# Two-layer decoder on one core: expert results written by token with indirect DMAs, and context units moved behind the expert tiles' branches

## The chip, the cores and the metric

The kernel runs on one core of a Trainium2 chip. The metric is the device time of one execution in microseconds (us), the median of several runs. TensorE (PE) multiplies matrices, VectorE (DVE), ScalarE (ACT) and GpSimd (POOL) do the rest of the arithmetic, and SyncE (SP) issues most DMAs. Each engine works through its own queue in order.

## What is computed

A decoder of two layers on x of 32 sequences x 128 tokens x 256 features, all in float32, with a context of the same shape. Each step adds its result to x, and each takes a layernorm of x first:

```python
x = x + L0_attn(layernorm(x))                    # latent attention, 16 heads
x = x + L0_xattn(layernorm(x), ctx)              # cross attention with position bias
x = x + L0_ffn(layernorm(x))                     # 8 experts, each token goes to the best 2
x = x + L1_attn(layernorm(x))                    # gated recurrence in chunks of 64, then an MLP
x = x + L1_xattn(layernorm(x), ctx)              # one head, keys and values of ctx
x = x + L1_ffn(layernorm(x))                     # ternary weights, 8-bit activations, 3-tap convolution
```

The expert step is the one that matters here. For each token, `w` are the softmax weights of the two best experts, and

```python
out = sum_e w[e] * (relu(x @ W1[e] + b1[e]) @ W2[e] + b2[e])   # 256 -> 1024 -> 256
```

The layer-1 cross attention needs keys `ctx @ W_lk.T + b_lk` and values `ctx @ W_lv.T + b_lv`, which depend on the inputs alone.

## The kernel before, in words

The program is written in a framework that orders each engine's instructions by its own time model and sets the semaphores. `keep_in_program_order` pins an instruction behind the one that was written before it on its engine; all matmuls and most transposes are pinned (helper `mm`, line 206, and `turned`, line 209), so TensorE's order is that of the text. Tracked dependencies are by tile and by region of a DRAM tensor.

**Attention, then routing.** x stays in SBUF throughout. After both attentions, `route` writes the normed rows to the DRAM tensor `xs` and picks two experts per token. `phase_c` sorts the 8192 pairs of token and expert into slots: each expert gets whole tiles of TS = 256 slots, 39 tiles at most (NT). Sixty-four small matmuls (line 781) turn the slots round into `who`, the token of each slot (line 786); `slots` (line 787) holds the two slots of each token.

**Contexts.** NU = 16 units of two sequences (U = 2, T = 256 tokens). `context(u)` gives three pieces: `load` (256 KB of transposed ctx into `cT`, line 666), `keys` (8 matmuls into `ck`, then ScalarE, line 677) and `values` (8 matmuls into `cv`, then VectorE, line 686, and a 512 KB store to the DRAM tensor `ckv`, line 690). Units 0 to 5 (CTX0 = 6) run before the expert tiles, units 6 to 15 in layer 1.

**Expert tiles.** For tile j: `brought` loads its expert's weights (2.2 MB into `moe`, line 800, two buffers) and gathers 2 x 128 rows of `xs` by `who` with indirect DMAs on GpSimd (`xr`, line 807, six buffers, so three tiles); `tokens` transposes them (copy at line 820); `first_layer` has 32 matmuls `h` and ReLU on ScalarE (line 832); `second_layer` has 32 matmuls `y` and the bias on VectorE (line 844), and stores the tile to its place in `ys` with one plain DMA (line 845). On TensorE the order is h of tile j, transposes of tile j+1, y of tile j. 36 tiles (`some`) always run, the last three only when `tiles > j`, which each engine tests on a register (loaded at line 862) in a branch. In the profiled execution 36 ran. The places of the three are filled with zeros before (line 854).

**Layer 1.** 16 units go through a chain of some 60 pieces each. PLAN gives the round of each piece, and each unit starts STEP = 11 rounds after the one before; eight or nine units are under way at a time. A unit begins with `gather` (four indirect DMAs from `ys` by `slots`, line 1054, pinned on GpSimd), and `added` (round 3, line 1063) adds them to x with the routing weights `rw`. Then come `d_stats`, `d_nb`, `d_norm` and `d_scaled` (a norm, its result `hn_d`), `d_flip` (transpose `pt_d`, copied by ScalarE into `hT_d`) and the projections `d_q` and so on, the scan (lines 1139 to 1145, with `u_d` of line 1113 on GpSimd), `m_y` (the output projection). The `kv_e` load of the context (line 1198) comes in round 32 and has two buffers, released by `lv_e` (line 1260). In the last step `f_taps` has a GpSimd addition (`z_f`, line 1320) between two ScalarE operations, and `f_out` stores x (line 1371).

The ten contexts of layer 1 are spread over its rounds by a table written by hand, three rounds for each unit:

```python
    CTX_ROUNDS = (
        (0, 0, 0), (0, 1, 1), (0, 2, 2), (0, 3, 3), (1, 4, 5), (2, 6, 7), (4, 9, 9), (6, 12, 12),
        (9, 14, 15), (12, 16, 17),
    )
```

In a round, contexts come ahead of the units' pieces. Their weights `wc` (line 1382, 512 KB) and those of the attention itself, `we` (line 942, 512 KB), are loaded at the start of layer 1.

Of the kernel before, what the change touches and what calls it, by code (L numbers as in the profile page):

```python
# [10 lines left out]
F32 = mybir.dt.float32  # L11
# [6 lines left out]
P = 128  # L18
# [4 lines left out]
G = 4  # L23
# [38 lines left out]
RV = {"b_vv": (0, D), "b_lv": (D, D), "br": (2 * D, NE), "bo": (2 * D + NE, D)}  # L62
RV_A = RV["bo"][0]


# [10 lines left out]
def decoder(ctx: ExitStack, tc: tile.TileContext, a: dict, out: bass.AP):  # L76
# [70 lines left out]
    def stats(src, name):  # L147
        st = small.tile([P, G, 6], F32, tag="st", name=f"st_{name}")
        mv = small.tile([P, G, 2], F32, tag="mv", name=f"mv_{name}")
        for i in range(G):  # L150
            V.bn_stats(st[:, i, :], src[:, i, :])
            V.bn_aggr(mv[:, i, :], st[:, i, :])
        return mv
# [66 lines left out]
    xs = dram.tile([NTOK, D], F32, name="xs")  # L220
    ys = dram.tile([NT * TS, D], F32, name="ys")
    U = 2
# [3 lines left out]
    rw = keepc.tile([P, 2, NB], F32, name="rw")  # L226
    slots = keepc.tile([P, 2, NB], I32, name="slots")
    wm = keepc.tile([P, 2], F32, name="wm")
    wq = keepc.tile([P, 2, 2048], BF16, name="wq")

    routed = ExitStack()
    keepr = routed.enter_context(tc.tile_pool(name="route", bufs=1))
# [12 lines left out]
    def attention():  # L245
        with tc.tile_pool(name="pa", bufs=2) as pool, tc.tile_pool(name="pa1", bufs=1) as keep:
# [329 lines left out]
            def route(g):  # L576
# [10 lines left out]
                for i in range(G):  # L587
                    for c in range(2):
                        mm(p3[:, i, :], xT[:, c, i * S : (i + 1) * S], W("r", 2)[:, c, :], c == 0, c == 1)
                sm = lambda t, sh=(P, G, NE): small.tile(list(sh), F32, tag=f"r_{t}", name=f"{t}_{n}", bufs=2)  # L590
                lg = sm("lg")
# [67 lines left out]
    def context(u, wcs, turned_tile, kv_tile):  # L659

        wc = wcs.rearrange("p (w c m) -> p w c m", w=2, c=2)
        t = {}

        def load():
            t["cT"] = turned_tile(f"cT_k{u}")
            nc.sync.dma_start(
                out=t["cT"], in_=a["ctxT"][:, u * T : (u + 1) * T].rearrange("(c p) t -> p c t", p=P)
            )

        def keys():  # L670
            t["kv"] = kv_tile(f"kvc_{u}")
            p = bank(f"ck_{u}").rearrange("p (c t) -> p c t", c=2)
            for c in range(2):
                for k in range(2):
                    mm(p[:, c, :], wc[:, 0, k, c * P : (c + 1) * P], t["cT"][:, k, :], k == 0, k == 1)
            for c in range(2):
                A.activation(
                    t["kv"][:, 0, c * T : (c + 1) * T], p[:, c, :], AF.Identity, bias=vec("b_lk")[:, c : c + 1]
                )

        def values():
            p = bank(f"cv_{u}").rearrange("p (i d) -> p i d", i=U)
            for i in range(U):
                for c in range(2):
                    mm(p[:, i, :], t["cT"][:, c, i * S : (i + 1) * S], wc[:, 1, c, :], c == 0, c == 1)
            V.tensor_tensor(
                t["kv"][:, 1].rearrange("p (i d) -> p i d", i=U), p,
                row("b_lv")[:, None, :].to_broadcast([P, U, D]), ALU.add,
            )
            nc.sync.dma_start(out=ckv[u], in_=t["kv"])  # L690

        return load, keys, values

    def load_d():
# [7 lines left out]
    def phase_c():  # L702
        with tc.tile_pool(name="pc", bufs=2) as pool, tc.tile_pool(name="pc1", bufs=1) as keep:
            wcs = keep.tile([P, E_W // 2], F32, name="wc")
# [61 lines left out]
            V.scalar_tensor_tensor(rowp, col, -float(P), sl, ALU.mult, ALU.add)  # L766
            pk = bank("tokens")
            F16 = mybir.dt.float16
            for t in range(0, NB, G):
                for j in range(2):  # L770
# [8 lines left out]
                    for i in range(G):  # L779
                        A.activation(c[:, i, :], c[:, i, :], AF.Copy, scale=conr("tok")[:, t + i : t + i + 1])  # L780
                        PE.matmul(
                            pk[:, :NJ], lhsT=o[:, i, :], rhs=c[:, i, :],
                            start=t + i + j == 0, stop=t + i == NB - 1 and j == 1,
                        )
            who = k("who", (NJ,), I32)
            V.tensor_scalar(who, pk[:, :NJ], float(NTOK // 2), None, ALU.add)
            V.tensor_copy(slots, sl)

            for u in range(CTX0):
                for piece in context(  # L790
                    u, wcs, lambda n: pool.tile([P, 2, T], F32, tag="cT", name=n, bufs=4),
                    lambda n: pool.tile([P, 2, U * D], F32, tag="kv", name=n, bufs=4),
                ):
                    piece()
            wf = keep.tile([P, 4096], F32, name="wf")

# [38 lines left out]
            def second_layer(t):  # L835
# [4 lines left out]
                for h in range(TS // P):  # L840
# [3 lines left out]
                    V.tensor_tensor(yt[:, h, :], y[:, :D], b2, ALU.add)  # L844
                nc.sync.dma_start(
                    out=ys[j * TS : (j + 1) * TS, :].rearrange("(h p) d -> p h d", h=TS // P), in_=yt
                )


            some = 2 * NTOK // TS + NE // 2  # L850
            none = keep.tile([P, TS // P * D], F32, name="none")
            GP.memset(none, 0.0)
            for j in range(some, NT):
                nc.sync.dma_start(
                    out=ys[j * TS : (j + 1) * TS, :].rearrange("(h p) d -> p h d", h=TS // P),
                    in_=none.rearrange("p (h d) -> p h d", h=TS // P),
                )
            tiles = nc.values_load(end_i[0:1, 0:1], min_val=0, max_val=NT)
# [8 lines left out]
            for j in range(some):  # L867
# [7 lines left out]
                if j == 3:  # L875
                    ternary(wf, keep)
                    for c in range(2):
                        for part, v in (
# [3 lines left out]
                            A.activation(part, part, AF.Copy, scale=vec(v)[:, c : c + 1])  # L882
            rest(some)
        return wd

    def ternary(wf, keep):
# [23 lines left out]
    PLAN = (  # L910
        (0, "gather0 gather1"), (1, "gather2 gather3"), (3, "added"), (4, "d_stats"), (5, "d_nb"),
        (6, "d_norm"), (7, "d_scaled"), (8, "d_flip"), (10, "d_q d_a"), (11, "d_k d_g d_scan1"),
        (13, "d_v d_q2"), (14, "d_rms d_scan2"), (15, "d_state"), (16, "d_gate"), (18, "m_y"),
# [10 lines left out]

    CTX0 = 6
    CTX_ROUNDS = (
        (0, 0, 0), (0, 1, 1), (0, 2, 2), (0, 3, 3), (1, 4, 5), (2, 6, 7), (4, 9, 9), (6, 12, 12),
        (9, 14, 15), (12, 16, 17),
    )

    def layer1(wd):
# [8 lines left out]
        with tc.tile_pool(name="pl", bufs=1) as pool, tc.tile_pool(name="pl1", bufs=1) as keep:  # L940
            wes = keep.tile([P, E_W // 2], F32, name="we")
            nc.sync.dma_start(out=wes, in_=a["we"][:, : E_W // 2])
            we = wes.rearrange("p (w c m) -> p w c m", w=2, c=2)
# [99 lines left out]
            def unit(u):  # L1043
# [4 lines left out]

                def gather(k):
                    t = u * U + k % U  # L1050
                    o["yr", k] = pool.tile([P, D], F32, tag="yr", name=f"yr_{t}_{k // U}", bufs=5)

                    tc.keep_in_program_order(
                        GP.indirect_dma_start(
                            out=o["yr", k], out_offset=None, in_=ys[:, :],
                            in_offset=bass.IndirectOffsetOnAxis(ap=slots[:, k // U, t : t + 1], axis=0),
                        )
                    )

                def added():  # L1060
                    for k in range(2 * U):
                        t, i = u * U + k % U, k % U
                        V.scalar_tensor_tensor(
                            x[:, i, :], o.pop(("yr", k)), rw[:, k // U, t : t + 1], x[:, i, :], ALU.mult, ALU.add
                        )

# [80 lines left out]
                def d_state():  # L1147
                    V.tensor_tensor(o["pre"], o["pre"], flat(o["qn"]), ALU.mult)
                    tc.keep_in_program_order(GP.tensor_tensor(o["pre"], o["pre"], o["v"], ALU.subtract))

# [223 lines left out]
                for k in range(4):  # L1374
                    for of in (gather, m_fc, m_out, f_h, f_z, f_taps, f_silu, f_top, f_round):
                        pieces[f"{of.__name__}{k}"] = partial(of, k)
# [4 lines left out]
            wcs = flat(sb("z", "wc1", 3, shape=(NHC, T)))[:, : E_W // 2]  # L1381
            nc.sync.dma_start(out=wcs, in_=a["we"][:, E_W // 2 :])
            between = {}
            for u in range(CTX0, NU):
# [9 lines left out]
            for t in range(STEP * (NU - 1) + PLAN[-1][0] + 1):  # L1394
                for piece in between.get(t, ()):
                    piece()
                for u in range(NU):
                    for name in pieces.get(t - STEP * u, ()):
                        units[u][name]()

    attention()
# [5 lines left out]
def laid_out(i):  # L1407
# [10 lines left out]
    def pv(v):  # L1418
        v = v.reshape(-1)
        if v.size < P:  # L1420
# [50 lines left out]
            np.broadcast_to(r, (P, P)),  # L1471
            np.arange(32)[None, :] * P + r[:, None] - 2048,
        ],
# [36 lines left out]
```

## Time and profile before

| | |
|---|---|
| median of 3 runs | 2038.31 us (2036.89 to 2038.47) |
| profiled execution | 2033.54 us |
| its span, first to last instruction | 2031.8 us |
| attention and routing | to 706 us |
| expert tiles, 36 of 14.25 us | 706 to 1220 us |
| layer 1, 16 units | 1220 to 2032 us |
| TensorE busy | 1818.1 us, 89% |
| VectorE, ScalarE, GpSimd busy | 1168.4 (58%), 1082.5 (53%), 437.2 us (22%) |
| indirect DMAs `xr` on GpSimd | 72, 949 ns each, 2.8 us to landing |
| indirect DMAs `yr` on GpSimd | 64, 70.3 us in all, 2.8 us to landing |
| plain stores `ys` | 36 of 256 KB, 2.2 us to landing |
| `kv_e` loads | 16 of 512 KB, 3.6 us to landing |

A busy TensorE is not TensorE at its peak: ends of matmuls are modelled. An entry "engine line <- releaser" says what ended an engine's idle time. Where a wait is put down to an engine or DMA that the waiting instruction doesn't read, another was meant.

### The profile page before, as it was taken

The page shows a single profiled execution, that of the slowest core. Times are in us where ns is not written, and L with a number is a line of the kernel's source. Part 1 is how long each engine was busy: PE and PEld are TensorE (multiplying, and loading weights), DVE is VectorE, ACT ScalarE, POOL GpSimd, SP SyncE. Part 2 cuts the span into 40 slices and gives each one's busy share as a digit, 9 for nine tenths or more (in the row PEclk, how much of TensorE's full clock was granted, in tenths as well). Part 3 has the DMA queues.
Part 4 walks back from the last instruction along what each step waited for, and adds up shares of the span by engine and source line. Part 5 has one row for each costly group of instructions (what it writes and reads, how often), then busy time and mean ns, then how long its engine had stood idle before and what let it go on. Part 6 is the DMA issues. An engine that isn't in the chain of part 4 may idle for free.

```text
span 2031.8 us, 35569 instructions
## 1 busy us (share of the span) xinstructions
PE 1818.1 (89%) x13496; PEld 1492.2 (73%) x13496; DVE 1168.4 (58%) x3716; ACT 1082.5 (53%) x2600; POOL 437.2 (22%) x445
## 2 busy tenths in 40 slices
PE   6999999899987899999999997899898888899863
PEld 4777766677665688888888886678777777777752
DVE  6877667788777512111111003446788777888797
ACT  4454548878785522222222222455666666667662
POOL 4100000000000111111111102333444444453221
PEclk9999999989998799999999998999999999999976
DMA  4000010111002845554655535101011010010000
GB/s 156 3 2 3 8 38 22 33 32 53 12 22 69 295 169 195 186 210 173 214 177 207 189 128 174 60 21 32 22 32 32 27 37 27 26 35 24 27 11 21
DMA packets 53965, 162.65 MB, mean 80 GB/s; under 512 B 5664, under 2 KB 36512, under 8 KB 48672
## 3 DMA queue, kind: packets, MB, share of 16 engines
q1 hardware_dynamic: 47264, 142.52, 19.8%
q0 software_dynamic: 6528, 17.83, 3.0%
q8 instruction: 108, 1.77, 0.3%
q14 instruction: 65, 0.53, 0.1%
HBM read 133.33 MB, written 27.00 MB: 79 GB/s over the span
## 4 chain that ended last, share of the span: by engine, by line
PE 49%; DVE 26%; ACT 10%; POOL 8%; issue 4%; DMA 3%; SPq 0%; POOLq 0%; DVEq 0%; ACTq 0%
PE h L206 12%; PE y L206 12%; ACT sd_b L531 4%; PE od_a L206 3%; DVE top_f L1333 3%; DMA yr<-ys,slots 2%; DVE sd_b L518 2%; PE st_a L206 2%; POOL z_f L1320 2%; PE et_b L209 2%; POOL u_d L1113 2%; PE ck L206 1%; DVE rd_a L497 1%; PE s_b L206 1%; PE q_a L206 1%
## 5 line engine op out<-in xcount | busy, mean ns | idle before, releaser
L832 ACT ACTIVATE hTs<-h,moe 128x256 f32<-128x256 f32 x288 | 136.6, 474 | 373.8 <-PE h L206 373.8
L206 PE MATMUL h<-xTs,moe 128*128 128x256 f32 x1152 | 254.7, 379 | 2.4 <-DVE xTs L820 2.4
L206 PE MATMUL y<-moe,hTs 128*128 128x256 f32 x1152 | 254.6, 379 | 0.0
L206 PEld LDWEIGHTS h<-xTs,moe 128*128 128x128 f32 x1152 | 218.7, 190 | 32.3 <-DVE xTs L820 2.7
L206 PEld LDWEIGHTS y<-moe,hTs 128*128 128x128 f32 x1152 | 216.2, 190 | 27.9
L531 ACT ACTIVATE sd_b<-sd_b,nan_b 128x128 f32<-128x128 f32 x512 | 173.8, 388 | 28.5 <-DVE nan_b L525 28.4
L807 POOL DMA_INDIRECT xr<-xs,who x72 | 68.3, 949 | 437.0 <-PE xs L209 397.7
L820 DVE COPY xTs<-xs 128x512 f32<-128x512 f32 x36 | 24.9, 691 | 233.8 <-PE xs L209 233.8
L844 DVE TENSOR_TENSOR yt<-y,moe 128x256 f32<-128x256 f32 x72 | 30.6, 425 | 215.6 <-PE y L206 215.6
L206 PE MATMUL m_m<-wd,sT_m 128*128 128x256 f32 x512 | 119.8, 382 | 3.4 <-ACT sT_m L1180 3.3
L206 PE MATMUL f_m<-hT_m,wd 128*128 128x256 f32 x512 | 118.4, 385 | 2.0 <-DVE x L1368 2.0
L518 DVE CUSTOM_DVE_ANT_0 sd_b<-nd_b,s_b 128x128 f32<-128x128 f32 x512 | 113.3, 280 | 5.3 <-PE s_b L206 5.3
L206 PEld LDWEIGHTS f_m<-hT_m,wd 128*128 128x128 f32 x512 | 96.4, 193 | 16.3 <-DVE x L1368 3.6
L206 PEld LDWEIGHTS m_m<-wd,sT_m 128*128 128x128 f32 x512 | 95.5, 191 | 16.8 <-ACT sT_m L1180 4.6
L1320 POOL TENSOR_TENSOR z_f<-z_f,e_f 128x508 f32<-128x508 f32 x64 | 70.8, 1106 | 171.3 <-ACT e_f L1318 113.3
L1314 DVE SCALAR_TENSOR_TENSOR z_f<-d_f,pv,z_f 128x254 f32<-128x254 f32 x128 | 64.3, 507 | 60.3 <-ACT z_f L1304 60.0
L1327 ACT ACTIVATE z_f<-z_f 128x512 f32<-128x512 f32 x64 | 40.3, 630 | 103.3 <-POOL z_f L1320 103.3
L497 DVE RECIPROCAL rd_a<-od_a 128x256 f32<-128x256 f32 x32 | 56.0, 1751 | 62.9 <-PE od_a L206 62.9
L544 POOL COPY dens_b<-den_b 128x256 f32<-128x256 f32 x32 | 12.8, 400 | 363.0 <-DVE den_b L542 210.1
L474 ACT ACTIVATE et_a<-st_a 128x512 f32<-128x512 f32 x128 | 66.5, 613 | 27.7 <-PE st_a L206 27.7
L444 DVE TENSOR_REDUCE nm<-s_a 128x4 f32<-128x512 f32 x128 | 79.1, 681 | 2.6 <-PE s_a L206 2.6
L1304 ACT ACTIVATE z_f<-d_f,pv 128x256 f32<-128x256 f32 x128 | 69.6, 590 | 20.1 <-DVE d_f L1299 20.1
(358 smaller groups left out, 4063.7 us busy)
## 6 DMA issues: line engine op xcount, KB each, us to landing
moe<-in_moe SPq DMA_DIRECT2D x36, 2180.0 KB, 8.2
ys<-yt SPq DMA_DIRECT2D x36, 256.0 KB, 2.2
ckv<-kvc SPq DMA_DIRECT2D x16, 512.0 KB, 3.2
kv_e<-ckv SPq DMA_DIRECT2D x16, 512.0 KB, 3.6
x<-in_x SPq DMA_DIRECT2D x8, 512.0 KB, 9.9
cT_b<-in_ctxT SPq DMA_DIRECT2D x8, 512.0 KB, 3.8
xs<-xn_c SPq DMA_DIRECT2D x8, 512.0 KB, 3.0
cT_k<-in_ctxT SPq DMA_DIRECT2D x16, 256.0 KB, 5.3
```

What stands on the lines that cost most here:

```text
L206: tc.keep_in_program_order(PE.matmul(out, lhsT=lhsT, rhs=rhs, start=start, stop=stop))
L444: V.tensor_reduce(nms[i % 2][:, at : at + 2 * (P - HD)].rearrange("p (e x) -> p x e", e=2)[:, :2, :], sp[r], AX.X, ALU.max, negate=True,)
L474: A.activation(et[:, r].rearrange("p j q -> p (j q)"), st[r], AF.Exp)
L497: V.reciprocal(rd, od[:, 2 * S :])
L518: V.tensor_tensor_reduce(sd[:, r, j, :], nd[:, i, :], sp[r][:, j, :], SLOPES[head(r, j)], -3e38, ALU.add, ALU.max, mx[:, 4 * r + j : 4 * r ...
L531: A.activation(sd[:, r, j, :], sd[:, r, j, :], AF.Exp, bias=nan[:, 4 * r + j : 4 * r + j + 1], accum_out=den[:, h : h + 1] if r % 2 else None,
L807: GP.indirect_dma_start(out=xr[h], out_offset=None, in_=xs[:, :], in_offset=bass.IndirectOffsetOnAxis(ap=who[:, q : q + 1], axis=0),)
L832: A.activation(hT[:, hc, :], p[:, :TS], AF.Relu, bias=b1[:, hc : hc + 1])
L1304: A.activation(o["z"][:, hc, :], o["d", k][:, j, :], AF.Identity, scale=cw[:, hc, 1:2], bias=cb[:, hc : hc + 1],)
L1314: V.scalar_tensor_tensor(z[:, :, 1:], d[:, j, :].rearrange("p (b t) -> p b t", b=U)[:, :, : S - 1], cw[:, hc, 0:1], z[:, :, 1:], ALU.mult, ...
L1320: GP.tensor_tensor(z[:, :, : S - 1], z[:, :, : S - 1], e.rearrange("p h (b t) -> p (h b) t", b=U)[:, :, 1:], ALU.add,)
L1333: V.tensor_reduce(o["top"][:, k, :], o["z"][:, 4 * k : 4 * k + 4, :].rearrange("p h t -> p t h"), AX.X, ALU.max, apply_absolute_value=True,)
```

## The change

Results by token. `ys` becomes a tensor of 3 x 4096 rows: a part for rows without a token, one for each token's first expert, one for its second. The token matmuls go to two banks, one for each choice, and some VectorE operations make `who` and `whither`, the row of `ys` that each slot's result belongs to. Each tile's plain store becomes two indirect writes on GpSimd, 128 rows each. The zero fill, `slots` and the gathers of layer 1 go; a unit's two blocks of 256 rows come with two plain loads on SP (`fetch`), into a pool of one buffer for each. The first unit's fetch stands right behind the branches.

Contexts. CTX0 becomes 11. Units 0 to 5 run before the tiles as they did. For units 6 to 10 the loads stand before the tiles (in the text; cT has five buffers instead of four), and keys and values behind the branches, before layer 1. Units 11 to 15 run in rounds 15 to 21 of layer 1 (loads in rounds 0 to 2, the last in 15), and in a round now come behind the units' pieces. `wc` is loaded again in round 0 and `we` in round 8. Stores of `ckv` are pinned; GpSimd's subtraction in `d_state` is no longer. Some small tiles get fewer buffers.

```diff
-    ys = dram.tile([NT * TS, D], F32, name="ys")
+    ys = dram.tile([3 * NTOK, D], F32, name="ys")
...
+    keepf = ctx.enter_context(tc.tile_pool(name="fetched", bufs=1))
...
-            nc.sync.dma_start(out=ckv[u], in_=t["kv"])
+            tc.keep_in_program_order(nc.sync.dma_start(out=ckv[u], in_=t["kv"]))
...
+    CTX_FIRST, CTX0 = 6, 11
+    first_made = []
+    def fetch(u):
+        y = []
+        for k in range(2):
+            y.append(keepf.tile([P, U, D], F32, tag=f"yr{k}", name=f"yr_{u}_{k}"))
+            at = (k + 1) * NTOK + u * T
+            tc.keep_in_program_order(
+                nc.sync.dma_start(out=y[k], in_=ys[at : at + T, :].rearrange("(i p) d -> p i d", p=P))
+            )
+        return y
...
-                            pk[:, :NJ], lhsT=o[:, i, :], rhs=c[:, i, :],
-                            start=t + i + j == 0, stop=t + i == NB - 1 and j == 1,
+                            pk[j][:, :NJ], lhsT=o[:, i, :], rhs=c[:, i, :],
+                            start=t + i == 0, stop=t + i == NB - 1,
...
+            two = k("two", (2, NJ))
+            for j in range(2):
+                V.tensor_copy(two[:, j, :], pk[j][:, :NJ])
+            tkn = k("tkn", (NJ,))
+            V.tensor_tensor(tkn, two[:, 0, :], two[:, 1, :], ALU.add)
+            late = k("late", (NJ,))
+            V.tensor_scalar(late, tkn, 0.0, None, ALU.is_gt)
+            V.scalar_tensor_tensor(tkn, tkn, float(NTOK // 2), late, ALU.add, ALU.subtract)
             who = k("who", (NJ,), I32)
-            V.tensor_scalar(who, pk[:, :NJ], float(NTOK // 2), None, ALU.add)
-            V.tensor_copy(slots, sl)
+            V.tensor_copy(who, tkn)
+            V.tensor_scalar(two, two, 0.0, float(NTOK), ALU.not_equal, ALU.mult)
+            V.scalar_tensor_tensor(tkn, two[:, 1, :], 2.0, tkn, ALU.mult, ALU.add)
+            V.tensor_tensor(tkn, tkn, two[:, 0, :], ALU.add)
+            whither = k("whither", (NJ,), I32)
+            V.tensor_copy(whither, tkn)
...
-            for u in range(CTX0):
...
+            for pieces in contexts[:CTX_FIRST]:
+                for piece in pieces:
                     piece()
+            for pieces in contexts[CTX_FIRST:]:
+                pieces[0]()
...
-                nc.sync.dma_start(
-                    out=ys[j * TS : (j + 1) * TS, :].rearrange("(h p) d -> p h d", h=TS // P), in_=yt
-                )
+                    q = j * (TS // P) + h
+                    GP.indirect_dma_start(
+                        out=ys[:, :], out_offset=bass.IndirectOffsetOnAxis(ap=whither[:, q : q + 1], axis=0),
+                        in_=yt[:, h, :], in_offset=None,
+                    )
...
             rest(some)
+            first_made.append(fetch(0))
+            for pieces in contexts[CTX_FIRST:]:
+                for piece in pieces[1:]:
+                    piece()
...
-        (0, "gather0 gather1"), (1, "gather2 gather3"), (3, "added"), (4, "d_stats"), (5, "d_nb"),
+        (0, "fetched"), (3, "added"), (4, "d_stats"), (5, "d_nb"), (6, "d_norm"), (7, "d_scaled"),
...
     CTX_ROUNDS = (
-        (0, 0, 0), (0, 1, 1), (0, 2, 2), (0, 3, 3), (1, 4, 5), (2, 6, 7), (4, 9, 9), (6, 12, 12),
-        (9, 14, 15), (12, 16, 17),
+        (0, 15, 15), (0, 16, 16), (1, 17, 17), (2, 19, 19), (15, 21, 21),
     )
...
-                def gather(k):
-                    t = u * U + k % U
-                    o["yr", k] = pool.tile([P, D], F32, tag="yr", name=f"yr_{t}_{k // U}", bufs=5)
-                    tc.keep_in_program_order(
-                        GP.indirect_dma_start(
-                            out=o["yr", k], out_offset=None, in_=ys[:, :],
-                            in_offset=bass.IndirectOffsetOnAxis(ap=slots[:, k // U, t : t + 1], axis=0),
-                        )
-                    )
+                def fetched():
+                    o["yr"] = fetch(u) if u else first_made.pop()
...
-                    tc.keep_in_program_order(GP.tensor_tensor(o["pre"], o["pre"], o["v"], ALU.subtract))
+                    GP.tensor_tensor(o["pre"], o["pre"], o["v"], ALU.subtract)
```

## The prediction

> **What bounds the kernel now.** I read the busy shares and slices first, then the table of stages, the chain of waits in order of time, and the waits and groups of single lines. The stage table (columns: stretch, its length, then busy us and instructions of PE, PEld, DVE, ACT and POOL, granted clock, DMA share, GB/s):
>
> ```profile
> 705.00:1220.00 515.00, 513.14 (x2446) 451.56 (x2446) 65.48 (x119) 136.60 (x288) 61.51 (x66) 1.00 0.52 184
> 1220.00:1231.00 11.00, 0.23 (x1) 0.26 (x2) 0.28 (x2) 0.00 (x0) 4.31 (x5) 0.71 0.77 242
> 1231.00:1300.00 69.00, 64.56 (x289) 54.78 (x290) 28.58 (x75) 28.22 (x55) 20.16 (x20) 0.97 0.38 133
> 1300.00:1900.00 600.00, 538.55 (x2770) 454.90 (x2769) 447.88 (x1147) 392.46 (x747) 254.60 (x225) 0.98 0.09 28
> 1900.00:2032.00 132.00, 75.08 (x401) 60.26 (x399) 104.33 (x246) 66.09 (x135) 24.54 (x23) 0.73 0.06 18
> ```
>
> The expert stage is TensorE from end to end: 513.1 of 515 us, 14.25 us for each of 36 tiles. Nothing outside TensorE's queue can shorten it. Layer 1 (1220 to 2032) leaves TensorE idle for 11 us at the seam, 4.4 until 1300, 61.5 from 1300 to 1900 and 57 in the drain of the last units. Only the first three, 77 us, can be reached by this change, since no gather and no context lies in the drain.
>
> The seam in the chain of waits (start, duration, what):
>
> ```profile
> 1219.69 0.44 DVE yt L844
> 1220.14 2.36 DMA ys<-yt
> 1222.91 0.71 issue
> 1223.62 7.12 DMA yr<-ys,slots
> 1230.77 3.75 PE ck L206 x8
> 1234.53 1.92 PE cv L206 x8
> 1236.45 1.73 PE ck L206 x8
> ```
>
> The name there misleads. `ck` doesn't read yr but cT and wc, and the DMA queue's timeline has those three loads behind the branch:
>
> ```profile
> 1222.03 0.36 SPq L942 DMA_DIRECT2D we<-in_we  x1
> 1222.76 0.35 SPq L1382 DMA_DIRECT2D wc<-in_we  x1
> 1223.16 13.69 SPq L666 DMA_DIRECT2D cT_k<-in_ctxT  x5
> ```
>
> So TensorE stands for 11.1 us because its first operands are only asked for at 1222, 512 KB of `we` in front. It then pays again: the first ck+cv pair takes 3.75 + 1.92 us, later pairs 1.73 + 1.73; that is 2.2 us lost after the pause, in which the granted clock was 0.71.
>
> In steady state (gathers of successive units start 43.75 us apart) the gathers hold up three engines. Among VectorE's waits from 1300 to 1900 (total us, times, longest):
>
> ```profile
> DVE x L1063 <- DMA yr<-ys,slots: 19.6, 25, 2.8
> ```
>
> Among the durations of one line in that window (min/median/max in ns) is a copy of four columns that takes 152 at best, but 1746 in the median:
>
> ```profile
> L1141 DVE COPY al_d<-first x14: 152/1746/1760, 1330.8 to 1870.9; 128x4 f32<-128x4 f32 x14
> ```
>
> The timeline shows why: it runs beside a gather's descriptor work on GpSimd. It also shows GpSimd's z_f coming only after four gathers, and ScalarE standing 5.4 us for it:
>
> ```profile
> 1694.96 1.69 POOL L1054 DMA_INDIRECT yr<-ys,slots  x1 [0.30 <-issue]
> ...
> 1696.07 1.75 DVE L1141 COPY al_d<-first 128x4 f32<-128x4 f32 x1
> ...
> 1696.68 1.09 POOL L1320 TENSOR_TENSOR z_f<-z_f,e_f 128x508 f32<-128x508 f32 x1
> ...
> 1697.81 0.63 ACT L1327 ACTIVATE z_f<-z_f 128x512 f32<-128x512 f32 x1 [5.41 <-POOL z_f L1320]
> ```
>
> **The change, part by part.** The sum is made against the profiled execution (2033.54 us, span 2031.8); the median of the runs is 4.8 us above it.
>
> *Routing (before 706).* About seven more small VectorE operations stand between the last token matmul and `who` (single ones in this stage take 0.15 to 0.25 us, so some 1.2 us). The gathers then start at 682 instead of 680.9; two descriptor issues and 2.8 us of landing bring the first tile in by about 687. TensorE asks for it at 703.3, after six contexts. Cost 0; without that cover, 1.2. Three zero stores (768 KB) go; the five later cT loads (1.28 MB) follow as slots come free, in a stage where DMA is busy 52%. I take 0, within 2 us either way: at 706 TensorE already waits 2.4 us for a VectorE busy with the ternary reduction, and that order may shift.
>
> *Expert stage.* Each tile's plain store (SP) becomes two indirect writes on GpSimd. No trace row has such a write; the nearest is the gather of the same size on the same queue: 945 ns each here, 1.25 apart, 2.8 from issue to landing. All writes name the whole of ys, so each may have to await the one before. GpSimd then spends at most 2 x (1.25 + 2.8) + 2 x 1.25 = 10.6 us of a 14.25 us tile. Behind a waiting write stand the next gathers, but six xr buffers put those three tiles ahead. TensorE's cost is 0. The lower bound is 0 too, as TensorE has no idle time here; the upper bound is in the third rival.
>
> *Seam.* The 11.1 us of waiting go: cT and wc of units 6 to 10 are in SBUF before the branch. What is late next? (a) The branch. [...] The trace shows such a step on SP: last store issued at 1220.14 + 0.37, next instruction at 1222.03, so 1.5 us. For TensorE it is hidden in the wait now. [...] I take 2.3. (b) Unit 0's input: last indirect write issued 1220.2, landed 1223.1, the fetch of two 256 KB blocks behind it at about 3.6 (a 512 KB kv_e load takes that) to 1227; from the first L1063 to the end of hn_d took 6.3 us (1231.3 to 1237.7), so 1233.5. Five contexts keep TensorE until 1222 + 5 x 3.46 = 1239.3, so this is hidden, by 6 us. (c) The other five contexts (17.3 us) move into rounds 15 to 21. Three of them sit where unit 0's scan leaves TensorE alone: v_d ended at 1269.7 and y_m started at 1280.1, 10.4 us, which three contexts fill today as well. Contexts keep their sum of 34.6 us, so this is neutral. Gain: 11.1 - 2.3 + 2.2 (the slow pair, if the short pause doesn't lower the clock) = 11.
>
> *Layer 1.* 64 gathers (70.3 us of GpSimd) leave, and 32 plain loads come on SP. fetch(u) is pinned behind the kv_e load of unit u-3 on SP. That one was issued at 1716.6 where the matching gathers came at 1734.8, so with 4 to 5 us of landing the data are there at 1722 and VectorE wants them at 1737: hidden by 15 us. Behind fetch in SP's queue stand output stores and kv_e loads; they gain or lose under 1 us of issue. (The smaller edits, fewer buffers for statistics and router tiles, pinned ckv stores and one pin less on GpSimd, cost 0: the tiles are written and read in order by the in-order VectorE, and SP has idle time throughout.) VectorE's 19.6 us of waiting therefore go. L1141's excess is 15.3 us for 16 less 16 x 0.152, 12.9 us, and a gather's descriptor work is what runs beside it. [...] I take half, 6. That makes 26 us on VectorE. The queues of ScalarE and GpSimd then take over part of the chain (VectorE waits 56.6 us for z_f L1304 and 22.0 for u_d L1113 in this window), so I count three quarters: 20 us. The lower bound is 0 (the waits move to those lines), the upper 50 of the 61.5 us TensorE is idle, if the freed GpSimd also ends ScalarE's 88 us of waiting for z_f. A loss is not excluded, since nearly every queue's order is laid anew; I allow 5 us.
>
> Sum: 0 + 0 - 11 - 20 = -31. Profiled execution 2002.5; median 2007.
>
> **The rivals.**
> *Only the seam* (0.20). Layer 1's period stays at 43.7 us because z_f, u_d and the single-file ScalarE set it: after all, VectorE's largest wait is z_f, not yr. Then -11: 2027.
> *A shorter period* (0.16). GpSimd without 5 us of gathers per unit frees z_f, ScalarE and with it the hT and xT_f copies that TensorE waits for (21.8 + 13.8 us). 45 us from layer 1: 1982.
> *Slower through the writes* (0.12). In the expert stage GpSimd becomes the bound, if an indirect write takes longer than a gather to land and each awaits the last. It decides from (14.25 - 2.5)/2 - 1.25 = 4.6 us of landing. At 5.5 a tile takes 16.0, 36 tiles cost 63 us more: 2007 + 63 = 2070. For it: the dependence on the whole tensor, and the empty rows, which all aim at one address. Against it: gather 2.8, plain store 2.2.
> *No effect* (0.07). The new order in rounds 15 to 21 and on the queues costs what the seam saves: 2038.
>
> **How the numbers follow.** Likeliest: 2007, chance 0.45, its own range 1994 to 2019. A measurement of this kernel can tell about 0.2% (4 us). Faster: 0.45 + 0.20 + 0.16 = 0.81. Same 0.07, slower 0.12. The range goes from 1980 (little of the shorter period is left out) to 2038, leaving out the writes' case and the tail of no effect.
>
> **What would show it.** Right: TensorE's pause at the seam near 2 us, its first context pair at 3.5 us; the tiles still 14.25 us apart; no wait at the line of `added`; starts of successive units 41.5 to 42.5 us apart. Wrong: tiles further apart with GpSimd waiting between writes; VectorE waiting for the fetch; the same 43.75 us with longer waits for z_f and u_d; flips of unit 0 later than the contexts' end.

## The result and the profile after

The kernel after took 2010.88 us (median of 4 runs, 2006.82 to 2014.75), the kernel before 2038.17 (4 runs), a ratio of 0.9867 [0.9847, 0.9887]. The forecast was 2007. The profiled execution of after is the longest of its four: 2014.75 us (span 2013.0), 18.8 less than the profiled one of before, where the medians differ by 27.3. The steps are judged below against the 18.8, as the forecast's sum was made from profiled executions.

The table of stages of after, for the same stretches (columns as in the prediction):

```profile
705.00:1220.00 515.00, 513.26 (x2440) 451.77 (x2441) 63.15 (x117) 136.35 (x288) 133.30 (x136) 1.00 0.52 185
1220.00:1231.00 11.00, 9.01 (x35) 7.34 (x34) 2.14 (x5) 1.15 (x3) 0.97 (x1) 0.84 0.23 74
1231.00:1300.00 69.00, 60.39 (x267) 51.24 (x266) 28.71 (x77) 30.46 (x54) 11.18 (x12) 0.93 0.43 150
1300.00:1900.00 600.00, 553.56 (x2848) 471.67 (x2847) 458.85 (x1186) 404.57 (x772) 189.61 (x178) 0.96 0.08 27
1900.00:2013.00 113.00, 61.85 (x320) 48.44 (x318) 87.97 (x202) 52.73 (x109) 20.80 (x20) 0.71 0.05 19
```

GpSimd's busy time moved from layer 1 (254.60 to 189.61 us in the fourth row) into the expert stage (61.51 to 133.30), where TensorE is as full as it was. The pause of the second row is mostly filled (9.01 us of 11), but the third row lost TensorE time: 60.39 us where there were 64.56. TensorE's timeline at the seam says why (start, duration, what, and in brackets the idle time ahead of it and what ended it):

```profile
1218.81 2.75 PE L207 MATMUL y<-moe,hTs 128*128 128x256 f32 x12
1223.55 3.65 PE L207 MATMUL ck<-cT_k,wc 128*128 128x256 f32 x8 [1.99 <-DVEq L898]
...
1240.85 1.89 PE L207 MATMUL cv<-wc,cT_k 128*128 128x256 f32 x8
1250.67 1.30 PE L210 MATMUL pt_d<-cst,hn_d 128*128 128x128 f32 x4 [7.93 <-ACT hn_d L1031]
1252.65 3.78 PE L207 MATMUL q_d<-hT_d,wd 128*128 128x256 f32 x8 [0.68 <-ACT hT_d L1043]
1256.22 2.64 PE L207 MATMUL a_d<-hT_d,wd 128*128 128x256 f32 x8
...
1275.10 1.89 PE L207 MATMUL y_m<-wd,yT_d 128*128 128x256 f32 x8
```

The 11.1 us in front of the contexts have become 2.0 in front and 7.9 behind, and the slow start is now paid twice (`ck` 3.65, `q_d` 3.78, where eight such matmuls otherwise end after 1.89 and follow 1.73 apart). ScalarE's timeline and SP's show what held unit 0:

```profile
1241.10 0.84 ACT L679 ACTIVATE kvc<-ck,pv 128x256 f32<-128x256 f32 x2 [2.66 <-issue]
1249.13 1.09 ACT L1024 ACTIVATE xn_d<-x,nb_d,rs_d 128x256 f32<-128x256 f32 x2 [7.19 <-DMA ckv<-kvc]
```

```profile
1242.82 0.34 SPq L1415 DMA_DIRECT2D we<-in_we  x1
1243.60 0.32 SPq L692 DMA_DIRECT2D ckv<-kvc  x1
1243.97 1.88 SPq L707 DMA_DIRECT2D yr<-ys  x2
```

`xn_d` of unit 0 reads no `kvc`; its statistics were ready at 1234.9. Its wait ends with the landing of the last store of `ckv`, 5.4 us after that store's issue between the load of `we` and the fetch of unit 1. The reading that the experiments below test: `xn_d` is written in layer 1's pool, that pool takes over memory of the stage before, and it opens only when the last store out of that stage has landed.

In steady state VectorE's largest wait is the one that the change was to remove. Its rows of the waits from 1300 to 1880 (total us, times, longest), where before had 19.6, 25, 2.8:

```profile
DVE x L1094 <- DMA yr<-ys: 34.6, 13, 4.0
DVE u_d L1175 <- POOL u_d L1144: 19.8, 7, 5.9
```

The copy beside the gathers, among the durations of one line (min/median/max in ns), and the indirect writes:

```profile
L1172 DVE COPY al_d<-first x14: 159/163/172, 1325.0 to 1850.8; 128x4 f32<-128x4 f32 x14
```

```profile
L887 POOL DMA_INDIRECT ys<-yt,whither x72: 969/987/1432, 720.2 to 1222.3; - x72
...
DMA to landing us min/median/max: 2.4/2.4/3.1
```

The `kv_e` loads of successive units start 42.2 to 42.6 us apart in most of the steady units; with two longer steps the mean of units 6 to 13 is 42.8 (43.9 before).

### The profile page after: what moved, and what is told of

It reads as the page before. It is cut to its first block, busy times and chain, and to the rows that moved or that the text cites. A ratio compares the mean times of both kernels' runs of the same rounds, so it can differ in the third digit from the quotient of the medians.

```text
span 2013.0 us, 35591 instructions
## 1 busy us (share of the span) xinstructions
PE 1826.2 (91%) x13496; PEld 1501.9 (75%) x13496; DVE 1165.6 (58%) x3724; ACT 1083.8 (54%) x2600; POOL 428.0 (21%) x452
## 5 line engine op out<-in xcount | busy, mean ns | idle before, releaser
L887 POOL DMA_INDIRECT ys<-yt,whither x72 | 71.6, 994 | 189.1 <-DVE yt L885 179.7
```

Of the source, the lines that this page charges most:

```text
L887: GP.indirect_dma_start(out=ys[:, :], out_offset=bass.IndirectOffsetOnAxis(ap=whither[:, q : q + 1], axis=0), in_=yt[:, h, :], in_offset=None,
```

## The experiments

My theory after reading the two traces: all the gain comes from results by token, the contexts' move gives nothing, since unit 0 is held at the seam; VectorE's wait for `yr` is a matter of order. The rivals were what the prediction had assumed (a seam of its own worth), a fetch that is merely issued late, and a gain that has nothing to do with GpSimd. Before was measured again beside each group of runs, and each ratio is taken against the median of its own group: 2040.13 us for `ctx_only`, `tok_only`, `no_late_store` and `added_pinned`; 2038.10 for `fetch_free`, `gathers_back` and the two `kv_apart_pinned`; 2036.94 for `pinned_free` and the two `kv_apart_free`.

**One half of the change each.** `ctx_only` is the kernel before with the contexts' part of the diff, without `keepf`, `fetch`, `who`/`whither` by two banks and the indirect writes:

```diff
+    CTX_FIRST, CTX0 = 6, 11
...
+            for pieces in contexts[CTX_FIRST:]:
+                for piece in pieces[1:]:
+                    piece()
...
-    CTX0 = 6
```

> Only the contexts are moved; gathers, plain stores and slots stay as before. Theory (the seam gains little, because unit 0's norm waits for the last context store and two contexts are still owed when m_y starts; the changed kernel's gain lies in the period of layer 1): 2033 to 2040, period of a unit 43.7. Rival, the prediction's own step (the seam is worth 11 us): 2027.

Measured: 2036.50 us, ratio 0.9990 [0.9976, 1.0004]. TensorE's timeline after its five contexts:

```profile
1254.74 1.30 PE L209 MATMUL pt_d<-cst,hn_d 128*128 128x128 f32 x4 [20.39 <-ACT hn_d L1004]
1256.72 3.78 PE L206 MATMUL q_d<-hT_d,wd 128*128 128x256 f32 x8 [0.68 <-ACT hT_d L1016]
```

The pause was moved behind the contexts and grew. Here the gathers, too, bring their rows into layer 1's pool: the first was issued at 1240.91 us, after 5.9 us of waiting for the landing of the last `ckv` store, and unit 0's norm follows its data. Contexts alone gain nothing that can be measured.

`tok_only` is the kernel after with the contexts where they had been:

```diff
-    CTX_FIRST, CTX0 = 6, 11
+    CTX_FIRST, CTX0 = 6, 6
...
-        (0, 15, 15), (0, 16, 16), (1, 17, 17), (2, 19, 19), (15, 21, 21),
+        (0, 0, 0), (0, 1, 1), (0, 2, 2), (0, 3, 3), (1, 4, 5), (2, 6, 7), (4, 9, 9), (6, 12, 12),
+        (9, 14, 15), (12, 16, 17),
```

> Only results by token: indirect writes, plain fetches; ten contexts in layer 1's rounds as before. Theory (period of layer 1): 2010 to 2019, period near 42.4, and VectorE waits for the fetches some 50 us in all. Rival, the prediction's split (11 of 31 us at the seam): 2018 to 2027. If the writes cost anything in the expert stage, tiles are more than 14.25 us apart.

Measured: 2010.57 us, ratio 0.9856 [0.9834, 0.9878]: all of the change's gain, with the seam's pause still there, and longer than in before. VectorE's waits for `yr` came to 36.4 us in all, where some 50 were expected.

```profile
1230.95 3.58 PE L207 MATMUL ck<-cT_k,wc 128*128 128x256 f32 x8 [15.40 <-DMA cT_k<-in_ctxT]
```

Counted from the end of the last `y`, unit 0's `y_m` comes after 64.3 us here, with all ten contexts done, and after 53.5 in the full change, with two (6.9 us) to come. The late contexts thus lead by 3.9 us at this point, but from the last `y` to the end the two kernels take 791.7 and 791.4 us: nothing of it is left.

**The landing at the seam.** `no_late_store` takes the late stores of `ckv` away: those of units 6 to 10 go out early, from unit 5's tile, so `ckv` of these five units holds unit 5's keys and values.

```diff
+            for u in range(CTX_FIRST, CTX0):
+                contexts[CTX_FIRST - 1][3](u)
...
-                for piece in pieces[1:]:
-                    piece()
+                pieces[1]()
+                pieces[2](False)
```

> The changed kernel without the five stores of context keys and values behind the branches; in their place the rows of units 6 to 10 are stored before the tiles, from unit 5's tile (so those units attend to unit 5's context: that part of the computation is replaced). Theory (layer 1's first tiles lie in memory that is only free when the last such store has landed, so unit 0's norm starts 6 us after its operands' last other user): ScalarE's first xn_d starts at 1235 to 1243 and not at 1249, TensorE's pause of 8 us after the contexts falls to under 3, time 2000 to 2006. Rival (something else holds the norm, or the pause is made up for later): first xn_d at 1249, or time within 3 us of 2011.

Measured: 2004.43 us, ratio 0.9822 [0.9802, 0.9843]. ScalarE's first normalisation came 7.3 us sooner than in after:

```profile
1241.87 1.09 ACT L1030 ACTIVATE xn_d<-x,nb_d,rs_d 128x256 f32<-128x256 f32 x2 [1.76 <-DVE bq L993]
```

TensorE waited 2.5 us instead of 7.9, and the time fell by 6 us by the medians and 9 by the ratios, as the theory had it (in after's profiled execution the first `ck` was slow besides, 3.65 us against 1.97 here). Without the late stores the wait is gone; whether their landing or their traffic made it is left to `kv_apart_pinned` below.

**VectorE's wait for the fetch.** In after, a unit's addition comes so early in VectorE's queue that its data are still on the way: in one unit the fetch is issued at 1702.9 us, and VectorE stands at the addition from 1703.7 to 1706.6. `added_pinned` keeps the addition at its place in the program:

```diff
-                            V.scalar_tensor_tensor(
+                            tc.keep_in_program_order(V.scalar_tensor_tensor(
```

> The changed kernel with the four additions of a unit pinned at their place in VectorE's queue (round 3), behind what the text has ahead of them; nothing else differs. Theory (the additions were ordered too early in that queue, right behind lv_e, and stand there about 3 us in each unit until the fetch has landed; z_f, ScalarE's copy hT_d and TensorE's q_d follow late): VectorE's wait for yr falls from 52 to under 15 us, TensorE's wait for hT_d from 28 to under 15, time 1990 to 2000. Rival (VectorE would have been idle in those places anyway): the wait goes over to z_f as before the change, time 2007 to 2015.

Measured: 2002.46 us, ratio 0.9809 [0.9789, 0.9829], between the two expectations. The wait for `yr` is gone; of the waits from 1300 to 1880, TensorE's are now

```profile
PE at_e L210 <- DVE at_e L1278: 27.2, 21, 2.5
...
PE q_d L207 <- ACT hT_d L1043: 2.4, 6, 1.0
```

where after had 27.2 for `q_d` and none for `at_e` among its largest. TensorE's wait changed its line; the units became 41.2 to 42.5 us apart, 41.9 in the mean of units 6 to 13.

`fetch_free` leaves the addition as it is and takes the pin from the two loads:

```diff
-            tc.keep_in_program_order(
-                nc.sync.dma_start(out=y[k], in_=ys[at : at + T, :].rearrange("(i p) d -> p i d", p=P))
-            )
+            nc.sync.dma_start(out=y[k], in_=ys[at : at + T, :].rearrange("(i p) d -> p i d", p=P))
```

> The changed kernel with the two loads of fetch no longer pinned in SP's queue. Theory (VectorE waits for yr because the addition stands early in VectorE's queue, whatever the load does): VectorE still waits for yr more than 20 us in all, and the time is 2003 to 2014 us. Rival (the pin is the cause: fetch stands behind the kv_e load of another unit and is issued too late): the wait for yr falls under 10 us in all and the time is 1995 to 2003 us.

Measured: 1993.08 us, ratio 0.9788 [0.9767, 0.9810], under the theory's range and the rival's, with 32.1 us of waits for `yr`, over the rival's 10. Neither was right, and SP's timeline says what happened:

```profile
1224.82 4.08 SPq L706 DMA_DIRECT2D yr<-ys  x3
1229.58 0.33 SPq L692 DMA_DIRECT2D ckv<-kvc  x1
1230.02 2.82 SPq L706 DMA_DIRECT2D yr<-ys  x2
1233.39 0.33 SPq L692 DMA_DIRECT2D ckv<-kvc  x1
1234.71 1.94 SPq L706 DMA_DIRECT2D yr<-ys  x2
...
1253.10 8.81 SPq L706 DMA_DIRECT2D yr<-ys  x4
```

All fetches, and with them all additions, have moved ahead to between 1225 and 1303 us; from 1300 to 1880 VectorE's wait for `yr` is 2.5 us. A steady unit has four VectorE instructions less (some 0.45 us each) and nothing to wait for, and the units are 39.9 us apart. TensorE paid for it at the seam, where it waited 12.7 us for unit 0 instead of 7.9:

```profile
1252.03 1.30 PE L210 MATMUL pt_d<-cst,hn_d 128*128 128x128 f32 x4 [12.70 <-ACT hn_d L1029]
```

`pinned_free` sets the fetch free and pins the addition, to tell the place of the loads from the place of the additions:

> The changed kernel with the two loads of fetch free in SP's queue, as in the run with fetch alone set free, but the addition pinned at its place in VectorE's order. Since each tile of yr has one buffer, the fetch of a unit then has to await the addition of the unit before it, in that unit's round. Theory (what shortened the units to 39.9 us was that all additions and fetches went ahead into the seam, so that a unit has four VectorE instructions less and nothing to wait for): with the additions back in their rounds the units are 41 to 42.5 us apart again and the time is 1998 to 2005 us, like the kernel with the addition pinned alone. Rival (it was the place of the fetch in SP's queue, in front of other loads and stores): units 40 us apart, 1990 to 1996 us.

Measured: 2001.11 us, ratio 0.9823 [0.9802, 0.9845], units 41.2 to 42.5 apart. So it is the additions, out of the steady units, that make 39.9. The loads were issued 8.5 us ahead of `kv_e` here (fetch at 1514.7, `kv_e` at 1523.2) and right behind it in `added_pinned`, and that is worth nothing by itself.

**Is it GpSimd?** `gathers_back` puts four gathers a unit back into layer 1 of after, in the places that they had in before; they read rows of `xs`, and nobody reads what they bring:

```diff
+                def gather(k):
+                    t = (u * U + k) % 16
+                    tc.keep_in_program_order(
+                        GP.indirect_dma_start(
+                            out=pool.tile([P, D], F32, tag="zr", name=f"zr_{u}_{k}", bufs=2), out_offset=None, in_=xs[:, :],
+                            in_offset=bass.IndirectOffsetOnAxis(ap=again[:, t : t + 1], axis=0),
+                        )
+                    )
```

> [...] Theory (layer 1 became shorter because GpSimd lost 64 instructions of 1.1 us and the four-column copy of al_d no longer stands beside their descriptor work): the copy is back at 1.7 us in the median, GpSimd is busy about 290 us in layer 1 instead of 223, ScalarE waits about 100 us for z_f instead of 81, successive units start 43.3 to 43.8 us apart, and the time is 2025 to 2036 us. Rival (the gain is that the data come by a plain load, ordered otherwise): units 42.4 apart, 2008 to 2015 us.

Measured: 2023.42 us, ratio 0.9932 [0.9915, 0.9948], just under the expected range; units 43.9 to 45 apart. Half of the gain (0.65 points of 1.33, some 13 us) came back with the gathers. The theory had the place right and the means wrong: the four-column copy stayed fast, as the durations of its line show, and ScalarE's wait for `z_f` rose only from 66.2 to 71.5 us (1300 to 1900).

```profile
L1183 DVE COPY al_d<-first x14: 156/164/172, 1321.0 to 1861.2; 128x4 f32<-128x4 f32 x14
```

What the waits show longer is the chain through GpSimd's queue. Its timeline in one unit:

```profile
1680.28 0.85 POOL L1015 TENSOR_TENSOR rs_e<-ve_e,mhalf 128x2 f32<-128x2 f32 x1
1681.14 1.05 POOL L1095 DMA_INDIRECT zr<-xs,again  x1
1682.49 0.99 POOL L1095 DMA_INDIRECT zr<-xs,again  x1 [0.30 <-issue]
1684.58 1.46 POOL L1095 DMA_INDIRECT zr<-xs,again  x1 [1.10 <-DMA zr<-xs,again]
1686.07 0.98 POOL L1015 TENSOR_TENSOR rs_d<-ve_d,mhalf 128x2 f32<-128x2 f32 x1
1687.25 1.01 POOL L1095 DMA_INDIRECT zr<-xs,again  x1 [0.20 <-DVE nb_d L1021]
1688.28 1.10 POOL L1362 TENSOR_TENSOR z_f<-z_f,e_f 128x508 f32<-128x508 f32 x1
```

`rs_d` stands behind three gathers and `z_f` behind the fourth. VectorE's waits for `rs_d` between 1300 and 1900, in after and then in `gathers_back`:

```profile
DVE nb_d L1019 <- POOL rs_d L1013: 2.5, 3, 0.9
DVE nb_d L1021 <- POOL rs_d L1015: 11.3, 9, 3.0
```

A part of it is the experiment's own: with two buffers, seven of the gathers waited for an earlier landing, 5.9 us in all. That the gathers' traffic has no part in it was not tested.

What came back is all of the steady units' gain: from unit 6 to unit 13 the `kv_e` loads are 43.9 us apart in before, 42.8 in after and 44.4 with the gathers back. The other half of the gain is in both kernels and lies in the first units: at the `kv_e` load of unit 6 both are 10 us ahead of before (1530.4 and 1530.6 against 1540.4), at that of unit 15 `gathers_back` still 10 and after 21. From unit 0's `y_m` to unit 4's, before took 134.9 us, and `gathers_back` 132.4 with two contexts (6.9 us) more. VectorE waited 16.6 us there for gathered rows in before, and 7.6 for the fetch in `gathers_back`, whose gathers bring what nobody awaits. So the likely cause is the waiting for the gathers' data, but no run separates it.

**A seam that opens sooner.** `kv_apart_pinned` is `added_pinned` with the `kv` tiles of contexts and layer 1 in one pool of two buffers (`vEO0` becomes a slice of a weight tile, to make room):

```diff
+    def kv_of(n):
+        return keepf.tile([P, 2, U * D], F32, tag="kv", name=n, bufs=2)
...
-                    lambda n: cpool.tile([P, 2, U * D], F32, tag="kv", name=n, bufs=4),
+                    kv_of,
```

> The changed kernel with two edits: the addition pinned in VectorE's order, and the key and value tiles of all contexts and of layer 1 in one pool of two buffers that lives through both stages, so that layer 1's pool need not await the landing of the last late store. Nothing is left out. Theory (unit 0's first normalisation was held by that landing, and this adds to the pinned addition): ScalarE's xn_d of unit 0 starts at 1240 to 1243 us instead of 1246.5 to 1249, TensorE waits under 3 us for unit 0's flips, and the time is 1993 to 1999 us, 4 to 9 under the pinned addition alone. Rival (two buffers instead of four make the late contexts wait for their stores, and the seam gives it back): waits of ScalarE for kvc in the seam, xn_d no earlier, 2000 to 2006 us.

Measured: 1997.27 us, ratio 0.9792 [0.9770, 0.9814]. Seam and time are as expected:

```profile
1241.35 1.09 ACT L1030 ACTIVATE xn_d<-x,nb_d,rs_d 128x256 f32<-128x256 f32 x2 [0.89 <-PE cv L207]
```

```profile
1242.89 1.06 PE L210 MATMUL pt_d<-cst,hn_d 128*128 128x128 f32 x4 [1.63 <-ACT hn_d L1037]
```

By the ratios the kernel is some 3 us under `added_pinned`, with intervals that overlap; from the last `y` to the end it took 774.4 us, and `added_pinned` 780.4. All five late stores are made here too, the last at 1242.1 us, when `xn_d` had already started; only the pool that unit 0 has to await is another. So it is the pool that the landing held up in after, and not the stores' traffic that slowed unit 0. The rival's waits were there (ScalarE stood 5.7 and 1.7 us for landings ahead of the third and fourth context), but TensorE went through the contexts without one.

`kv_apart_pinned_tern` pins the first ternary reductions too (`tc.keep_in_program_order(V.tensor_reduce(` at L933):

> As the last, and the first ternary reductions of layer 1's weights pinned in VectorE's order, so that they no longer stand ahead of the first expert tile's copies. Theory (TensorE's wait of 3.6 us ahead of the first expert tile comes from two of them in front of the first xT copy, and makes the first matmuls slow): the wait is under 2 us, the first h matmuls take about 7.2 us instead of 8.9, and the time is 2 to 4 us less than with the pinned addition and the kv tiles apart, 1990 to 1996 us. Rival (it is elsewhere in VectorE's queue that they then stand, and the time is the same within 1.5 us).

Measured: 1995.22 us, ratio 0.9783 [0.9766, 0.9799]. A miss in its mechanism: TensorE still waited ahead of the first tile (4.27 us, 4.31 without the pin), and its matmuls were as slow, since one reduction still stands between the transposes and the copy. Its row:

```profile
704.59 8.86 PE L207 MATMUL h<-xTs,moe 128*128 128x256 f32 x32 [4.27 <-DVE xTs L867]
```

The first `h` began 2.35 us sooner than without the pin, but the contexts ahead of it had ended 2.32 us sooner already, so the pin didn't do that. The 2 us less lie inside the intervals.

`kv_apart_free` joins `fetch_free` with the pool of two buffers:

> Fetch and addition both free, and the key and value tiles of all contexts and of layer 1 in one pool of two buffers. Nothing is left out. With fetch free alone TensorE waited 12.7 us at the seam for unit 0's flips, though VectorE had unit 0's statistics by 1232.7 us; ScalarE's xn_d was held to 1250.5 us by the landing of the last late store. Theory (that landing is the only thing in the way): xn_d before 1241 us, a wait of TensorE under 3 us, units still 39.9 us apart, and 8 to 11 us less than with fetch free alone: 1982 to 1986 us. Rival (the loads that now crowd the seam, fifteen fetches beside we and cT, become what holds unit 0 or the late contexts): a wait of 5 us or more in the seam, 1987 to 1994 us.

Measured: 1988.43 us, ratio 0.9756 [0.9738, 0.9773]: under `fetch_free`, with intervals that just touch, but short of the theory. The rival's mechanism is in ScalarE's timeline:

```profile
1237.51 0.84 ACT L682 ACTIVATE kvc<-ck,pv 128x256 f32<-128x256 f32 x2 [2.58 <-DMA ckv<-kvc]
1241.94 0.84 ACT L682 ACTIVATE kvc<-ck,pv 128x256 f32<-128x256 f32 x2 [3.59 <-DMA ckv<-kvc]
1242.67 1.08 ACT L1028 ACTIVATE xn_d<-x,nb_d,rs_d 128x256 f32<-128x256 f32 x2
```

The stores of the contexts go out between the fetches, and with two buffers each context awaits the landing of the one two before it; unit 0 stands behind the last of them. TensorE waits 4.5 us instead of 12.7.

`kv_apart_free_tern` adds the pin of the reductions to that:

> As the last, and the first ternary reductions of layer 1's weights pinned in VectorE's order. In the pair with the addition pinned this ended the expert stage about 2.5 us earlier. Theory (the two edits have nothing to do with each other): 1.5 to 3 us less than without the pin, 1979 to 1984 us. Rival: the order of VectorE's work in the seam shifts with it and the time is the same within 1 us or longer.

Measured: 1985.46 us, ratio 0.9742 [0.9727, 0.9757]. The first `h` started at 705.53 us instead of 705.38, so the pin did nothing at its place, and the 3 us are within the two intervals. From the last `y` to the end both kernels took 767.5 us, and `fetch_free` 769.9. The two kernels with fetch free and the tiles apart are the fastest seen, some 1.1 to 1.3 points of ratio under the change.

## Why the prediction was right, and where it was wrong

The sum was -31; the medians differ by 27.3 and the profiled executions by 18.8. A profiled execution is one of several that scatter by some us: after and `added_pinned` have the same text up to the contexts, and yet their first context began at 679.20 and 676.60 us. By the sum's terms:

- *Routing and expert stage, 0.* Measured +1.9. The tiles are 14.25 us apart and TensorE is full, as forecast. The first `h` began at 706.74 us (before 706.51) after a wait of 3.6 us, with two reductions of 4.5 us ahead of its copy on VectorE, and its 32 matmuls took 8.86 us instead of 7.17. The forecast had named that order as one that may shift. In other kernels with the change's routing the first `h` began between 702.4 and 706.9 us, so the 1.9 can't be told from scatter.
- *Seam, -11.* This step failed in its part (b): "Five contexts keep TensorE until 1222 + 5 x 3.46 = 1239.3, so this is hidden, by 6 us." The data of unit 0 were indeed there in time (statistics at 1234.9), but the first tile written in layer 1's pool had to await the landing of the last context's store, a wait that the step didn't list because no tile of unit 0 has anything to do with `kvc`. From the end of the last `y` to unit 0's `y_m` took 60.4 us before and 53.5 after, and in after two contexts (6.9 us) were still to come at that point: the gain is about 0. `ctx_only` (0.9990 [0.9976, 1.0004]) shows that the move gains nothing alone, and `no_late_store` and `kv_apart_pinned` show what stood in its way.

  Its part (a) took 2.3 us for the branch. No run shows that figure; what after showed is 1.99 us on TensorE. What ended that wait is VectorE's semaphore at the branch: VectorE was done with the last bias at 1222.0, took the branch at 1222.8 and signalled at 1223.4. TensorE's own branch row lasted 3.4 us, from 1217.5 to 1220.9, under the last tile's matmuls, and its timeline shows no other wait at the branch. The slow pair, which was to go, stayed in this execution (3.65 us); in seven of the other kernels with late contexts and fetch it was gone (1.97).

  Part (c) misread the trace of before: between unit 0's `v_d` and `y_m` stand two contexts, not three, and 2.6 us of waiting. In after three contexts fill that place and TensorE doesn't wait there; the 53.5 us have this in them. The rows of before:

```profile
1267.81 1.89 PE L206 MATMUL v_d<-hT_d,wd 128*128 128x256 f32 x8
...
1270.39 1.89 PE L206 MATMUL ck<-cT_k,wc 128*128 128x256 f32 x8
...
1273.85 1.89 PE L206 MATMUL ck<-cT_k,wc 128*128 128x256 f32 x8
...
1280.09 1.99 PE L206 MATMUL y_m<-wd,yT_d 128*128 128x256 f32 x8 [2.63 <-DVE yT_d L1154]
```

- *Layer 1, -20.* The remainder of the 18.8 is -20.7. From the last `y` to the end, which leaves the scatter ahead of it out, before took 812.2 us, after 791.4 and `tok_only` 791.7, so two executions agree on it. The period, 42.4 us in the median of the steady steps, lies in the forecast's 41.5 to 42.5; the mean, 42.8, is just over it. Its size was right; its makeup was not, and that is luck. "VectorE's 19.6 us of waiting therefore go" failed: the fetch was taken as hidden by 15 us, but the addition was ordered right behind it, and the wait rose to 34.6 us. Against that, GpSimd gave more than was counted: 11 to 13 us by `gathers_back` (from the last `y` to the end it took 802.1 us), and another 10 came in the first units, whose cause is open. Of the 12.9 us of L1141 nearly all returned (163 ns for the median copy), where the forecast had taken half, 6 us; no run shows that half. But `gathers_back` shows that this copy isn't what the period hangs on: with the gathers back it stays at 164 ns and the units still lengthen to 44 us, by the waits through `rs_d` and `z_f` behind gathers in GpSimd's queue. The waits of ScalarE for GpSimd's `z_f` (85.4 to 66.2 us from 1300 to 1880) had been counted only as an upper bound.

So it is partly luck that the median came within 4 us of the forecast. By the profiled executions the sum was 12 us too large; that of before lay 4.8 us under its median and that of after 3.9 over its own, and this made up for most of it. And two errors of the sum, 11 us at the seam and the wait for `yr`, met a larger gain on GpSimd. Among the rivals, "only the seam" has its opposite: only layer 1. "Slower through the writes" decides from a landing of 4.6 us; it was 2.4, and GpSimd waited for an earlier write 6.7 us in the whole stage.

## What to carry to other kernels

When work is put behind a stage's end to fill a pause, list what the next stage's first tile waits for by memory as well as by data: here the landing of the filler's last store held the pool that reuses its place, and ScalarE stood 7.2 us for it. A load that is taken from another engine doesn't free its consumer (here VectorE's wait for the data rose from 19.6 to 34.6 us); look where the consumer then stands in its own in-order queue, and ask whether load and consumer can move out of the repeated part altogether: here that was worth another 0.8 points of ratio, beside the 1.3 of the change. A gather that nobody waits for is not free either: four a unit cost some 13 us here, with small operations waiting behind them on their engine.

## What the runs showed of the hardware

- An indirect write of 128 rows of 1 KB cost GpSimd 0.99 us and landed after 2.4, the gather of the same size in before 0.95 and 2.8.
- A pause at TensorE may cost twice. Ahead of the first expert tile, waits of 1.00 to 2.44 us left the first 32 `h` at 7.17 us (before, `ctx_only`, `tok_only`), and waits of 3.63 to 5.18 made them 8.80 to 8.86 (after, `added_pinned`, `no_late_store` and the four `kv_apart` kernels). But after 7.9 us of idle in after, and likewise after 1.6 in `kv_apart_pinned`, the group of eight `q_d` matmuls behind four flips took 3.78 us instead of 1.89, and behind the branch's 1.99 us the first `ck` took 3.65 in after but 1.97 in seven of the other kernels with late contexts and fetch. So the length of the pause alone doesn't decide. In after the granted clock went with the slow groups: it was 0.50 from 708.2 to 711.0 us, within the first `h`, from 1223.6 to 1226.9, under the slow `ck`, and from 1247.5 to 1257.6, under the flips and `q_d`; it was 1.00 from 1227.0 to 1247.4, between the last two, and in before throughout the first `h`. What lowered it behind one pause and not behind an equal one was not shown.
